# Layer 0: the two stores of each finished block of x1 go out on SyncE's queue instead of ScalarE's

## The chip, the cores and the metric

The kernel runs on one core of one Trainium2 chip. The metric is device time in microseconds (us): the median of three runs, 2891.63 us for the kernel before (2888.98 to 2893.01).

A core has five engines that run their own instruction streams and meet at semaphores: TensorE (PE; its weight loads are shown apart as PEld), VectorE (DVE), ScalarE (ACT), GpSimd (POOL) and SyncE (SP). In this kernel DMA transfers are issued from three of these streams: SP, ACT and POOL. An instruction that issues a DMA stands in its engine's stream like any other: what is written behind it on that engine waits for it to be issued.

## What is computed

The input x is (4, 16, 256, 256) float32: 4 images of 16 channels. Two layers follow each other, each with a residual:

```python
x = x + _L0_conv_ref(_gn(x), L0_conv_conv_w, L0_conv_conv_b)
x = x + _L1_conv_ref(_gn(x), L1_conv_base_weight, L1_conv_spline_weight,
                     L1_conv_spline_scaler, L1_conv_bias_weight)
```

`_gn` is a group normalization over 8 groups of 2 channels. Layer 0 computes, for each channel and pixel, 25 logits by a 3x3 convolution, a softmax over these 25, and the weighted sum of the 5x5 neighbourhood:

```python
out = conv_general_dilated(x, conv_w, padding='SAME') + conv_b
weights = softmax(out.reshape(N, C, 25, H, W), axis=2)
return einsum('ncuij,ncuij->ncij', unfold_5x5(x), weights)
```

Layer 1 is a 3x3 convolution over SiLU of its input and over eight cubic B-spline bases of it. It needs the group statistics of layer 0's result, called x1 here.

## The kernel before

**Layer 0** (`layer0`) works in strips: 128 image rows by 32 columns, all 16 channels; 4 images x 2 row halves x 8 strips = 64 strips. The variable n is the strip, j the column in it. A strip is done in 8 steps of 4 columns. In each step

- PE makes the logits of 4 columns with 2 matmuls for each (L974 from the tile am, L978 from an), 400 numbers per pixel, into PSUM tiles lg of two columns; three such tiles exist;
- ACT takes the exponential of each lg into a tile e (L997); four e tiles exist;
- POOL multiplies e with the pixels u (L1002) into e's second half;
- DVE sums both halves over the 25 neighbours into nd, numerator and denominator (L813), one step behind.

At the end of a strip nd becomes y, the quotient, on ACT (`seed`, L827 and L829: exp(-ln)) and DVE (`divide`, `refine`, `quotient`; L833, L837, L844). These small pieces are not done at once but put on a list with a number of steps to wait (`after`, `step`), so that they fall into later steps.

**Loads.** `load_im` brings am (four DMAs, L750) and an (one, L758) for 16 columns, half a strip; each has two buffers, so that a half's load waits until PE has finished the half before the one in hand. `load_u` (L771) brings u for a strip, `load_xc` (L791) the block's own x. All these are on SP's queue. Beside the strips the generator `normalize` prepares the next image: it loads xp (L321), normalizes on ACT (L373, L386), transposes on PE, and stores normalized rows and columns to DRAM on SP's queue (L329, L343; zero borders L312). One piece of it is drawn in each step with `next(ahead)`, after `step()`.

**The block of x1.** Four strips make a block of 128 columns (BS = 4), 16 blocks in all. When the last strip of a block has its quotient, `apply` adds y to xc with an accumulating DMA on POOL's queue (L851). Six steps later the statistics for layer 1 begin (`statistics`, L876: for each of 8 groups, one group a step, two activations with a running sum on ACT), and seven steps later `store` writes the block to DRAM, twice, since layer 1 reads x1 with its channels doubled: two DMAs of 1024 KB each (L913), in pieces of 512 bytes. For 15 of the 16 blocks they are on ACT's queue; for the last block (`n == len(strips) - 1`), which is finished strip by strip on POOL (L861), they are on POOL's. Counting the steps from the block's last strip n, the store falls into the step j = 12 of strip n + 3, on ACT behind the second group's statistics and ahead of that step's `seed` (L827).

**Order.** At the end of `layer0` a pass (`in_order`) ties every instruction to the one before it on the same engine, so each engine runs its instructions in the order in which they are written. On SP that is, around a store's step: the load_im called at j = 0; what `normalize` emits in the steps j = 0, 4, 8; the store's place, j = 12; what `normalize` emits there; then at j = 16 the next load_im, load_u and load_xc. Semaphores and the waits on them are made by the framework. Layer 1's instructions may begin behind marks near the end of layer 0 (`marks`; SP's is set at strip 60, ACT's at 61).

**Layer 1** (`layer1`) runs over 64 units of 16 rows: it loads x1 (xta, xtb, xtc, L1084; sla, slb, slc, L1097; yo, L1106) on SP's queue, computes spline features on ACT, DVE and POOL into ring, and the convolution on PE (L1304, L1313).

Of the kernel before, what the change touches and what calls it, by code (L numbers as in the profile page):

```python
# [34 lines left out]
def conv_preact_kernel(  # L35
# [12 lines left out]
    nc = tc.nc  # L48
# [430 lines left out]
    with tc.tile_pool(name="prep0", bufs=2) as prep, tc.tile_pool(  # L479
# [147 lines left out]
        for b in range(B):  # L627
            st = stat.tile([P, G, NH * (GC if b == 0 else 1), 6], F32, name=f"st0_{b}", tag=f"st0{min(b, 1)}")
            for hf in range(NH):
                n = b * NH + hf  # L630
# [90 lines left out]
    def layer0(shift):  # L721
# [4 lines left out]
        with tc.tile_pool(name=f"prep{arm}", bufs=2) as prep, tc.tile_pool(  # L726
# [11 lines left out]
            strips = [(b, hf, s) for b in range(B) for hf in range(NH) for s in range(NST)]  # L738
# [109 lines left out]
            def apply(n, y):  # L848
                xc = kept_blocks[n // BS]
                if not alone(n):  # L850
                    nc.gpsimd.dma_start(  # L851
                        xc.rearrange("p c w -> p (c w)"), y.rearrange("p c w -> p (c w)"),
                        accum_op=ALU.add,
                    )
                    for g in range(G):
                        after(6 + g, statistics, n, xc, g)
                    after(7, store, n, xc)
                    return
                w0 = n % BS * SW
                v = xc[:, :, w0 : w0 + SW]  # L860
                nc.gpsimd.tensor_add(v, v, y[:, :, w0 : w0 + SW])  # L861
                seeds[1:] = [newest(POOLE)]
                if n == len(strips) - 1:
                    store(n, xc)
                    after(1, last_statistics, n, xc)
# [40 lines left out]
            def store(n, xc):  # L906
                b, hf, s = strips[n]
                c0 = s * SW + SW - CX
                v = x1s[b][:, W : W + H * W].rearrange("c (p w) -> p c w", w=W)

                queue = nc.gpsimd if n == len(strips) - 1 else nc.scalar
                for h in range(2):
                    queue.dma_start(  # L913
                        v[hf * P : (hf + 1) * P, h * C : (h + 1) * C, c0 : c0 + CX], xc
                    )
# [521 lines left out]
```

## Time and profile before

The profile is one execution, 2885.0 us, its span (first to last instruction) 2883.2 us.

| what | before |
|---|---|
| median of 3 runs | 2891.63 us (2888.98 to 2893.01) |
| profiled execution / its span | 2885.0 / 2883.2 us |
| busy: PE, DVE, ACT, POOL | 2712.4, 2777.8, 2143.5, 2663.9 us |
| DVE, share of the span | 96% |
| SP's queue (q1): packets, MB, share of 16 DMA engines | 267876, 626.67, 70.2% |
| ACT's queue (q10): the same | 61920, 31.46, 3.8% |
| POOL's queue (q0): the same | 7664, 32.23, 5.4% |
| issues of x1s<-xc on ACT / on POOL | 30 / 2, 1024 KB each |

The page cuts the span into 40 slices of 72 us and gives the busy share of each engine in tenths:

```profile
PE   4699899999999999999999999996899999999998
DVE  7699899999999999999999999999999999999996
ACT  6566777667677567776665555647999999999995
POOL 4399899999999999999999999999899999999995
DMA  9877899879899778898886666766787878787883
```

Slices 1 and 2 are preparation (statistics of x, weights). Layer 0 follows, from about 123 us (POOL's first L1002) to about 2010 us (DVE's last L813), slices 2 to 28; the rest is layer 1. In layer 0 three engines, PE, DVE and POOL, are at 9 nearly everywhere, and ACT is at 5 to 7. A "9" is 90% or more: the row doesn't say which of the three has no time left. In the profile's lists of groups and waits, "L913 ACTq" is a DMA issue in ACT's stream; an idle time put down to "issue" is one in which the engine waited for nothing that the profile shows.

### The profile page before, as it was taken

The page shows a single profiled execution, that of the slowest core. Times are in us where ns is not written, and L with a number is a line of the kernel's source. Part 1 is how long each engine was busy: PE and PEld are TensorE (multiplying, and loading weights), DVE is VectorE, ACT ScalarE, POOL GpSimd, SP SyncE. Part 2 cuts the span into 40 slices and gives each one's busy share as a digit, 9 for nine tenths or more (in the row PEclk, how much of TensorE's full clock was granted, in tenths as well). Part 3 has the DMA queues.
Part 4 walks back from the last instruction along what each step waited for, and adds up shares of the span by engine and source line. Part 5 has one row for each costly group of instructions (what it writes and reads, how often), then busy time and mean ns, then how long its engine had stood idle before and what let it go on. Part 6 is the DMA issues. An engine that isn't in the chain of part 4 may idle for free.

```text
span 2883.2 us, 39200 instructions
## 1 busy us (share of the span) xinstructions
PE 2712.4 (94%) x14282; PEld 1499.2 (52%) x14282; DVE 2777.8 (96%) x1821; ACT 2143.5 (74%) x2737; POOL 2663.9 (92%) x1096
## 2 busy tenths in 40 slices
PE   4699899999999999999999999996899999999998
PEld 3466566666666666666666556664233343323222
DVE  7699899999999999999999999999999999999996
ACT  6566777667677567776665555647999999999995
POOL 4399899999999999999999999999899999999995
PEclk7799999999999999999999999998899999999999
DMA  9877899879899778898886666766787878787883
GB/s 286 258 230 228 265 283 294 265 225 270 248 283 272 237 218 245 252 290 246 250 252 186 198 191 192 205 207 203 221 261 239 260 244 258 237 264 244 256 246 104
DMA packets 337663, 692.96 MB, mean 240 GB/s; under 512 B 29554, under 2 KB 254276, under 8 KB 287092
## 3 DMA queue, kind: packets, MB, share of 16 engines
q1 hardware_dynamic: 267876, 626.67, 70.2%
q0 software_dynamic: 7664, 32.23, 5.4%
q10 hardware_dynamic: 61920, 31.46, 3.8%
q8 instruction: 115, 1.88, 0.3%
q14 instruction: 88, 0.72, 0.1%
HBM read 533.16 MB, written 121.15 MB: 227 GB/s over the span
## 4 chain that ended last, share of the span: by engine, by line
DVE 35%; PE 28%; POOL 11%; issue 10%; ACT 7%; DMA 6%; SPq 2%; DVEq 0%; ACTq 0%; POOLq 0%
DVE nd L813 25%; PE lg L974 13%; POOL e L1002 10%; PE yp L1304 9%; PE lg L978 4%; DVE ring L181 3%; DVE s L178 3%; PE yp L1313 2%; ACT xtb L1139 1%; DMA xtb<-x1s 1%; DVE r1a L1148 1%; ACT xta L1139 1%; DMA xin<-in_x_dram 1%; DMA xta<-x1s 1%; ACT xtc L1139 1%
## 5 line engine op out<-in xcount | busy, mean ns | idle before, releaser
L1002 POOL TENSOR_TENSOR e<-e,u 128x1600 f32<-128x1600 f32 x512 | 1804.8, 3756 | 70.7 <-ACT e L997 53.3
L974 PE MATMUL lg<-wm,am 128*128 128x400 f32 x4096 | 1737.3, 505 | 75.0 <-ACT e L997 61.8
L813 DVE TENSOR_REDUCE nd<-e 128x128 f32<-128x3200 f32 x512 | 1759.2, 3480 | 37.4 <-POOL e L1002 37.1
L978 PE MATMUL lg<-wn,an 96*128 96x400 f32 x2048 | 1350.7, 660 | 1.8 <-DMA an<-hsl 1.8
L997 ACT ACTIVATE e<-lg 128x800 f32<-128x800 f32 x1024 | 845.5, 839 | 576.0 <-PE lg L978 465.1
L974 PEld LDWEIGHTS lg<-wm,am 128*128 128x128 f32 x4096 | 766.8, 193 | 384.2 <-ACT e L997 79.8
L1304 PE MATMUL yp<-ring,wt 128*32 128x512 f32 x6144 | 721.2, 594 | 31.1 <-DVE ring L181 30.6
L978 PEld LDWEIGHTS lg<-wn,an 96*128 96x128 f32 x2048 | 389.3, 190 | 314.1 <-issue 10.5
L1304 PEld LDWEIGHTS yp<-ring,wt 128*32 128x32 f32 x6144 | 224.2, 109 | 494.6 <-issue 432.9
L1161 POOL TENSOR_TENSOR s1b<-s1b,r1a 128x1024 f32<-128x1024 f32 (+1 forms) x96 | 192.4, 2034 | 0.0
L1161 POOL TENSOR_TENSOR s1a<-s1a,r1a 128x1024 f32<-128x1024 f32 (+1 forms) x96 | 191.9, 2027 | 0.0
L181 DVE SCALAR_TENSOR_TENSOR ring<-s,s1a 128x1024 f32<-128x1024 f32 x132 | 156.7, 1212 | 0.9
L181 DVE SCALAR_TENSOR_TENSOR ring<-s,s1b 128x1024 f32<-128x1024 f32 (+1 forms) x128 | 153.8, 1227 | 0.3
L876 ACT ACTIVATE z<-xc,nrm 128x256 f32<-128x256 f32 x240 | 143.8, 599 | 4.0
L1161 POOL TENSOR_TENSOR s1a<-s1a,r1b 128x512 f32<-128x512 f32 (+2 forms) x68 | 119.3, 1778 | 0.0
L1161 POOL TENSOR_TENSOR s1b<-s1b,r1b 128x512 f32<-128x512 f32 x64 | 114.6, 1814 | 0.0
L178 DVE SCALAR_TENSOR_TENSOR s<-xta,cb,s 128x1024 f32<-128x1024 f32 (+2 forms) x90 | 112.4, 1274 | 0.5 <-DMA xtc<-x1s 0.4
L1157 POOL TENSOR_TENSOR s1a<-r1b 128x1536 f32<-128x1536 f32 (+1 forms) x31 | 86.5, 2790 | 24.9 <-ACT r1b L1146 24.9
L178 DVE SCALAR_TENSOR_TENSOR s<-xtb,cb,s 128x1024 f32<-128x1024 f32 (+2 forms) x85 | 107.3, 1289 | 0.4 <-ACT s L175 0.4
L178 DVE SCALAR_TENSOR_TENSOR s<-xtc,cb,s 128x1024 f32<-128x1024 f32 (+2 forms) x85 | 107.1, 1287 | 0.0
L175 ACT ACTIVATE s<-xta,cb 128x1024 f32<-128x1024 f32 (+2 forms) x90 | 96.4, 1085 | 12.4 <-DVE ring L181 11.0
L1157 POOL TENSOR_TENSOR s1b<-r1b 128x1536 f32<-128x1536 f32 (+1 forms) x32 | 86.2, 2695 | 20.5 <-ACT r1b L1146 20.5
(211 smaller groups left out, 2255.0 us busy)
## 6 DMA issues: line engine op xcount, KB each, us to landing
am<-hst SPq DMA_DIRECT2D x508, 259.8 KB
u<-hs SPq DMA_DIRECT2D x64, 1440.0 KB
an<-hsl SPq DMA_DIRECT2D x127, 519.5 KB
xta<-x1s SPq DMA_DIRECT2D x40, 1024.0 KB
xtb<-x1s SPq DMA_DIRECT2D x40, 1024.0 KB
xtc<-x1s SPq DMA_DIRECT2D x40, 1024.0 KB
x1s<-xc ACTq DMA_DIRECT2D x30, 1024.0 KB
hs<-hsp SPq DMA_DIRECT2D x32, 576.0 KB
```

Of the source, the lines that this page charges most:

```text
L175: nc.scalar.activation(s, t, AF.Square, scale=-0.5, bias=cb)
L178: nc.vector.scalar_tensor_tensor(p, t, cb2, s, ALU.subtract, ALU.mult)
L181: nc.vector.scalar_tensor_tensor(f, p, 0.0, q, ALU.min, op)
L813: nc.vector.tensor_reduce(nd[:, :, :, j : j + JG].rearrange("p t c j -> p t j c"), e.rearrange("p t j m c d -> p t j c m d"), AX.XY, ALU.add,)
L876: nc.scalar.activation(z, v, f, scale=nrm[b][:, 0, g : g + 1], bias=nrm[b][:, 1, g : g + 1], accum_out=st1[b][:, t, g, columns_of(n) : col ...
L974: nc.tensor.matmul(lg[:, i, :NL], lhsT=am[:, o : o + P], rhs=wm.rearrange("p m c d -> p (m c d)"), start=True, stop=False,)
L978: nc.tensor.matmul(lg[:, i, :NL], lhsT=an[:, o : o + P], rhs=wn.rearrange("p m c d -> p (m c d)"), start=False, stop=True,)
L997: nc.scalar.activation(ev, lg[:, :, :NL], AF.Exp)
L1002: nc.gpsimd.tensor_tensor(e[:, 1].rearrange("p j m c d -> p j (m c) d"), e[:, 0].rearrange("p j m c d -> p j (m c) d"), uv, ALU.mult,)
L1157: nc.gpsimd.tensor_tensor(s1(n, a, z), r1(n, a, z), r1(n, a, z), ALU.mult)
L1161: nc.gpsimd.tensor_tensor(s1(n, a, z), s1(n, a, z), r1(n, a, z), ALU.mult)
L1304: nc.tensor.matmul(yp[t * M : (t + 1) * M], lhsT=wt[:, d, e].rearrange("p r o -> p (r o)"), rhs=ring[:, r0 + t * RT + d : r0 + t * RT + d ...
```

## The change

```diff
@@ -908,7 +908,7 @@
                 c0 = s * SW + SW - CX
                 v = x1s[b][:, W : W + H * W].rearrange("c (p w) -> p c w", w=W)
 
-                queue = nc.gpsimd if n == len(strips) - 1 else nc.scalar
+                queue = nc.gpsimd if n == len(strips) - 1 else nc.sync
                 for h in range(2):
                     queue.dma_start(
                         v[hf * P : (hf + 1) * P, h * C : (h + 1) * C, c0 : c0 + CX], xc
```

The 30 stores of the first 15 blocks are issued in SP's stream. They move the same bytes between the same places, called in the same step of the program. The last block's two stay on POOL.

## The prediction

> **What bounds the kernel now.** I first read the cost groups, to see which engine of layer 0 has no time to spare. The columns are busy us, mean ns of one, then the idle time in front and who ended it.
>
> ```profile
> L1002 POOL TENSOR_TENSOR e<-e,u 128x1600 f32<-128x1600 f32 x512 | 1804.8, 3756 | 70.7 <-ACT e L997 53.3
> L813 DVE TENSOR_REDUCE nd<-e 128x128 f32<-128x3200 f32 x512 | 1759.2, 3480 | 37.4 <-POOL e L1002 37.1
> ```
>
> Both run once per four columns (a step) in about 3.5 us, so either could be the bound. The windows view of most of layer 0 decides: columns are busy time of PE, PEld, DVE, ACT, POOL, then clock and DMA share.
>
> ```profile
> 470.00:2000.00 1530.00, 1478.80 (x5183) 963.50 (x5181) 1520.18 (x601) 992.19 (x1625) 1495.38 (x464) 0.99 0.80 235
> ```
>
> DVE is idle for 1530.0 - 1520.2 = 9.8 us out of 1530, POOL for 35. The DVE timeline agrees: in a strip (8 steps) DVE has eight sums plus the three quotient operations (L833, L837, L844), together 28.94 us, which is what most strips last. **A stall of ACT, PE or POOL is therefore worth only what it makes DVE idle.** POOL's gaps are mostly its own spare time (8 x 3.48 = 27.9 against 28.94).
>
> Second, the store. The view by tile of xc (min/median/max ns), and ACT's timeline at the fifth block:
>
> ```profile
> L913 ACTq DMA_DIRECT2D x1s<-xc x30: 366/1074/5172, 313.2 to 1954.4; - x30
> ...
> 784.24 4.14 ACTq L913 DMA_DIRECT2D x1s<-xc  x2
> 784.74 0.19 ACT L876 ACTIVATION_READ_ACCUMULATOR z<-xc,nrm 128x1 f32 x1
> 788.43 0.60 ACT L827 ACTIVATE r<-nd 128x512 f32<-128x512 f32 x1 [3.50 <-issue]
> ...
> ACT r L827 <- issue: 49.9, 15, 5.0
> ```
>
> The first store of a pair issues in 0.37 us; the second holds ACT's queue for 1.76 to 5.17 us, and L827, which is next, starts when it lets go. Fifteen pairs cost ACT 49.9 us.
>
> Third, SP. Its waits (total, times, longest), and its timeline around the same store:
>
> ```profile
> SPq L750 <- PE lg L978: 845.2, 110, 12.8
> SPq L771 <- DMA x1s<-xc: 63.1, 11, 8.9
> SPq L343 <- DMA x1s<-xc: 44.3, 5, 13.9
> SPq L750 <- DMA x1s<-xc: 41.1, 10, 8.0
> ...
> 771.52 0.63 SPq L758 DMA_DIRECT2D an<-hsl  x1
> 776.80 0.38 SPq L321 DMA_DIRECT2D xp<-in_x_dram  x1
> 777.77 0.33 SPq L312 DMA_DIRECT2D hst<-zero  x1
> 782.11 9.00 SPq L750 DMA_DIRECT2D am<-hst  x4
> 791.22 1.20 SPq L758 DMA_DIRECT2D an<-hsl  x1
> 793.96 0.34 SPq L771 DMA_DIRECT2D u<-hs  x1
> ```
>
> SP mostly waits for PE to free an am buffer (845 us). It also waits 148 us for these stores, though am, u and hst read nothing of x1s: the records show eight completion semaphores taken in turn by the DMAs of both queues (the store at 784.24 and the am load issued at 790.60 carry the same one), so a late store holds a later load. Here the fourth am load comes 7 us after the third.
>
> **What the change removes.** All 15 pairs leave ACT: 49.9 us of stall. What that is worth is the idle time of DVE after each store. I asked DVE's waits in the 45 us after each of the 15 issues: in order 7.9, 3.0, 0, 0, 0.4, 0, 0, 0.7, 1.6, 2.0, 0, 0.5, 0, 0, 0. A typical one:
>
> ```profile
> 1243.02 17.05 DVE L813 TENSOR_REDUCE nd<-e 128x128 f32<-128x3200 f32 x5
> 1261.29 3.49 DVE L813 TENSOR_REDUCE nd<-e 128x128 f32<-128x3200 f32 x1 [1.21 <-POOL e L1002]
> ```
>
> Nine us after the store of 1250.5, DVE runs dry for 1.21 us; ACT had stood for 3.74, and queued e tiles covered the other 2.5. At seven other blocks cover was complete. In the first block not all is the store's. DVE's big gap there is 6.28 us; ACT waited 8.7 us for an xp load (L373) just before, which had used up the cover, and the store's share is its 3.74 us. The second (3.0) is loads held by the store's semaphore as much as ACT. The later ones sum to 0.44 + 0.71 + 1.63 + 2.25 + 0.54 = 5.6, with one small gap of the 1367.7 block just past the window, from DVE's timeline. Sum: 3.7 + 3.0 + 5.6 = **12.3 us**.
>
> A rule speaks against more than nothing: the Trainium skill, "DMA: Bandwidth & Descriptors", section "Issuing engines are not separate DMA queues", says that all issuers share the same 16 DMA engines, and that the choice of issuer saves only sequencer time, "usually small relative to the DMA itself". By the rule the edit is worth about 0. By the row the issue is not small: up to 5.2 us, while the packets of a pair end 8.4 to 11.9 us after its issue. I take the row for ACT's time and the rule for bandwidth: no byte moves faster.
>
> **What it adds on SP.** Thirty issues. By the step counters a block's store falls at column 12 of the strip after next but one, in program order behind the loads called at column 0 and ahead of those called at column 16 (am, an, u, xc). Three prices:
>
> (a) The wait for the accumulate of y into xc, which ACT paid earlier through its statistics. POOL issues it 23 to 33 us before today's store; it lands in
>
> ```profile
> DMA to landing us min/median/max: 8.8/12.7/14.3
> ```
>
> so at the latest some 9 us before, typically 11. SP has issued `an` 13 to 21 us before the store in 12 blocks (8 to 11 in three) and then has at most a few small DMAs (six column stores in four blocks) until PE frees the am buffer 2 to 3.5 us before it. So the wait lies inside SP's wait for PE: 0. If that cover failed, the next half's am, an, u and xc would all wait behind it, and PE for them.
>
> (b) Issue time: 0.37 + 1.76 us (ACT's rows where SP issued nothing at the same time), at most 0.37 + 5.17. With it the pair is done before PE's release in the eleven blocks without column stores, else about 2 us after it. A half takes PE 14 us, loads issue in 3.1 us, and an `an` load lands 5.7 us after issue (chain at 1026.61). So about 5 us are free: 0. Bounds: 0 to 15 x 2 us if nothing covered it.
>
> (c) Order of data. The same page, "Queues, rings and completion order", says that a DMA engine takes turns between queues but consumes each ring in order: am will now stand behind up to 2 MB of stores instead of alternating with them. By that rule, a pair issued 4 us before today's time in the worst blocks holds am's data to about +4.5, and it lands near +10 to +12 of today's store, where PE wants it at +12. By the row, today the semaphore makes it worse: at 1015.9 the am loads are issued at +5.8 to +10.1 and `an` lands at +16.4, PE waits, and DVE still has no idle time. So by both: 0 or a small gain. Elsewhere the stores run 5 to 11 us earlier than now and are over when am comes.
>
> Below nothing: the 148 us of SP's waits on stores mostly go. They cost DVE little today, already counted in block two.
>
> **The end of layer 0.** The last SP store moves to about 1942, the first load of layer 1 is at 1974. DVE waits 4.56 us at 2009.7 for ACT's last logarithm; ACT, free of a 3.95 us stall at 1954, may come earlier: gain 0 to 4.6. ACT is again paced by PE by then, so I take 0.
>
> What is late next is DVE itself, then the xp loads (idle at 300 to 312 and at 1700).
>
> **Sum.** -12.3 + 0 + 0, and I leave 1 us for small new gaps: -11.3. The profiled execution took 2885.0 us (span 2883.2), so its like is 2873.7 (span 2872). The median shown is 2891.6, within 0.3% of it; taken from that: **2880.3 us**. Its own range is 2873 to 2886.
>
> **Rivals.** *Hidden anyway.* DVE's gaps come back: statistics (16 activations of 0.6 us and their reads per block) overload ACT in the same steps, and PE's share of the cover is not larger. For it: blocks with a short second issue (1.76) still gave POOL gaps of 0.5 to 2.7. Against it: DVE had none there. With half or less of 12.3 returned: 2886 to 2892, say 2888.
>
> *Loads late behind the stores.* One queue, in order: the stores keep am, an and u back. Place: the first blocks (300 to 470), where DMA share is 0.94, and the four with six column stores ahead. It decides once the loads land more than 16.4 us after today's store time, which the trace shows to be harmless; that needs the pair's transfer to take 16 us or more rather than 8.4 to 11.9. Three blocks late by 2.7 us beyond that point make 8 us of DVE idle, and one more wait for xp like the first block's 6 us; less the 5.6 still gained at the later blocks, that is +8.4: 2900. Against it: SP's 845 us of waiting and the earlier issue.
>
> *The whole stall counts.* If POOL's and ACT's time were the bound, all 49.9 us would go: 2842. DVE's zero idle at seven stores speaks against it.
>
> *The change does nothing* is not open: only the last block's pair is on POOL, which stays.
>
> **Chances.** Forecast 0.60, hidden anyway 0.22, loads late 0.15, whole stall 0.03. A difference of under 0.2% (5.8 us) can't be told from no change here. Faster 0.63, same 0.22, slower 0.15. The range reaches from 2870 (12.3 + 4.6, and the 4 us by which runs differ) to 2896, most of the late-load case left out.
>
> **What would show it.** Right: no "issue" idle in front of L827; L913 on SP, issued 3 to 13 us before the matching ACT statistics; SP's waits for x1s<-xc near 0; DVE's gaps after stores gone, those at 300 to 312 and 1700 left; DVE's sums end near 1998 instead of 2009.7. Wrong: waits of PE for am or an, or of POOL for u, longer than now (8.0, 6.4 and 15.9 us); SP's store rows above 5 us; DVE idle in layer 0 not under 15 us (21.6 now); or layer 1 longer than 874 us from DVE's last sum to the end.

## The result, and the profile after

The changed kernel takes **2865.24 us** (median of four runs, 2861.58 to 2870.83), the kernel before, measured with it, 2890.31 us (2887.43 to 2893.01). The ratio is 0.9915, with a 95% interval of 0.9896 to 0.9934: 25.1 us faster, 19 to 30 by the interval. The forecast was 2880.3 us, 11.3 us faster. The profiled execution took 2861.6 us (span 2859.8, before 2883.2: 23.4 less); a second profiled execution of the same kernel, taken with the experiments, has a span of 2863.2 us (20.0 less). So two profiles of one kernel differ by 3.4 us here, and the four runs range over 9.

The issue itself went as foreseen. ACT's timeline at the fifth block no longer has the store; L827 follows the statistics at once. The columns are start, duration, then engine, line and tiles.

```profile
773.83 0.19 ACT L876 ACTIVATION_READ_ACCUMULATOR z<-xc,nrm 128x1 f32 x1
773.93 0.58 ACT L827 ACTIVATE r<-nd 128x512 f32<-128x512 f32 x1
```

The store stands in SP's timeline instead, 10 us before the place that it had beside these statistics:

```profile
759.29 0.68 SPq L758 DMA_DIRECT2D an<-hsl  x1
760.07 0.53 SPq L321 DMA_DIRECT2D xp<-in_x_dram  x1
760.65 0.50 SPq L312 DMA_DIRECT2D hst<-zero  x1
763.92 6.40 SPq L913 DMA_DIRECT2D x1s<-xc  x2
770.41 5.13 SPq L750 DMA_DIRECT2D am<-hst  x4
775.64 0.55 SPq L758 DMA_DIRECT2D an<-hsl  x1
776.29 0.53 SPq L771 DMA_DIRECT2D u<-hs  x1
```

The second issue of a pair is longer on SP than it was on ACT, 4.1 to 8.65 us (the view by tile: min, median, max ns over both issues of a pair), and all four am loads now follow without a break. SP has the time: its wait for PE in front of am stays in the hundreds of microseconds, and its 148 us of waits for the stores are gone from the list.

```profile
L913 SPq DMA_DIRECT2D x1s<-xc x30: 359/2754/8647, 295.5 to 1919.3; - x30
```

```profile
SPq L750 <- PE lg L978: 883.3, 110, 12.0
```

The costliest groups after. DVE's sums take as long as before; the idle time in front of them was 37.4 us and is 20.5, of which some 15 are the start of layer 0. ACT's idle time is now put down mostly to DVE.

```profile
L1002 POOL TENSOR_TENSOR e<-e,u 128x1600 f32<-128x1600 f32 x512 | 1806.0, 3818 | 45.0 <-ACT e L997 27.8
L813 DVE TENSOR_REDUCE nd<-e 128x128 f32<-128x3200 f32 x512 | 1757.9, 3489 | 20.5 <-POOL e L1002 20.5
L997 ACT ACTIVATE e<-lg 128x800 f32<-128x800 f32 x1024 | 810.3, 835 | 627.2 <-DVE nd L813 504.3
```

That last number is the main sign of what happened. ACT's waits in layer 0 (total us, times, longest), before:

```profile
ACT e L997 <- PE lg L978: 451.7, 548, 3.6
ACT e L997 <- DVE nd L813: 102.4, 69, 4.6
```

and after:

```profile
ACT e L997 <- DVE nd L813: 504.3, 333, 2.4
ACT e L997 <- PE lg L978: 100.1, 126, 2.2
```

Before, ACT mostly waited for PE to make a new lg: nothing lay ready in front of it. After, it mostly waits for DVE to free an e tile: all four e tiles are full. The work in hand ahead of DVE is a stock; it stood near empty and now stands near full.

**Where the microseconds went.** A strip without any loss takes DVE 28.94 us, from its first sum to the next strip's first sum. What a strip takes beyond this I call its excess; unlike the idle time that the profile names, it contains every loss. It is worked out from the starts of the 512 rows of L813.

| place | before | after | after, second execution | predicted gain | gain (mean of both) |
|---|---|---|---|---|---|
| strips 5 to 11 (first two stores) | 14.1 | 4.9 | 8.6 | 6.7 | 7.35 |
| strips 12 to 52 | 9.0 | 0.9 | 1.0 | 5.6 | 8.05 |
| strip 53 | 3.2 | 0.5 | 0.5 | 0 | 2.7 |
| last sum's start to the end of the run | 876.9 | 874.5 | 874.4 | 0 | 2.45 |
| ahead of the first sum | 126.5 | 125.6 | 125.5 | 0 | 0.95 |

The gains add up to 21.5 us, against 21.7 between the spans (mean of 23.4 and 20.0). The profiled execution of the kernel before is itself 5 us under that kernel's median, so 3.4 of the 25.1 us have no place in this table. The last row is not the change's: no store of x1 has been issued by then, and over the profiled executions of all runs this time lies anywhere between 121.5 and 128.7 us. Three of these places deserve a look at their rows.

*Strips 12 to 52.* The windows view of this stretch (length, then busy time of PE, PEld, DVE, ACT, POOL, then clock, DMA share, GB/s), before and after:

```profile
490.00:1650.00 1160.00, 1125.40 (x3967) 734.55 (x3967) 1153.81 (x440) 778.01 (x1293) 1135.01 (x348) 0.99 0.84 247
```

```profile
490.00:1650.00 1160.00, 1142.14 (x4006) 729.45 (x4005) 1159.54 (x446) 767.28 (x1295) 1147.26 (x351) 1.00 0.84 249
```

DVE's idle time falls from 6.2 to 0.5 us: 5.7, and the prediction said 5.6. But the excess falls by 8.05. The other 2.3 us were never shown as idle. In the kernel before, DVE's timeline has at 1273:

```profile
1273.27 6.87 DVE L813 TENSOR_REDUCE nd<-e 128x128 f32<-128x3200 f32 x2
1280.56 10.43 DVE L813 TENSOR_REDUCE nd<-e 128x128 f32<-128x3200 f32 x3 [0.42 <-POOL e L1002]
```

One sum lasts 3.49 us in its row; two that follow each other from a full stock take 6.87, so they start 3.38 apart. The three behind the gap take 10.43, so they start 3.47 apart, and no idle time stands between them: DVE follows POOL, which has just the next e ready. That is 0.09 us a sum that the idle column can't show.

*Strip 53.* The prediction put the idle time "at 1700" down to xp. The kernel before has there:

```profile
1683.30 17.05 DVE L813 TENSOR_REDUCE nd<-e 128x128 f32<-128x3200 f32 x5
1700.71 3.49 DVE L813 TENSOR_REDUCE nd<-e 128x128 f32<-128x3200 f32 x1 [0.36 <-POOL e L1002]
1704.11 0.68 DVE L833 TENSOR_TENSOR nd<-nd,r 128x512 f32<-128x512 f32 x1
1706.92 3.49 DVE L813 TENSOR_REDUCE nd<-e 128x128 f32<-128x3200 f32 x1 [2.13 <-POOL e L1002]
```

and the kernel after, in the same strip:

```profile
1665.14 20.47 DVE L813 TENSOR_REDUCE nd<-e 128x128 f32<-128x3200 f32 x6
1685.50 0.70 DVE L833 TENSOR_TENSOR nd<-nd,r 128x512 f32<-128x512 f32 x1
1686.10 3.51 DVE L813 TENSOR_REDUCE nd<-e 128x128 f32<-128x3200 f32 x1
```

POOL does a piece of image statistics there in both kernels (L206 and L207, 0.48 + 1.66 us before, 0.43 + 1.66 after). With a full stock DVE doesn't feel it; with an empty one it waits 2.5 us. The store that emptied it had been issued at 1601, 100 us earlier, far outside the 45 us that the prediction looked at.

ACT's stall of 5 us is not all that emptied it. All lg tiles were full, so PE stopped too, and behind that stop its granted clock was halved. PE's rows of L974 alone in the kernel before, around the store of 1601, and the windows view behind the stop (the clock is the number after the five busy times):

```profile
1602.92 0.84 PE L974 MATMUL lg<-wm,am 128*128 128x400 f32 x2
1608.85 1.70 PE L974 MATMUL lg<-wm,am 128*128 128x400 f32 x2 [4.91 <-ACT e L997]
1610.68 1.53 PE L974 MATMUL lg<-wm,am 128*128 128x400 f32 x2
1612.26 0.83 PE L974 MATMUL lg<-wm,am 128*128 128x400 f32 x2
```

```profile
1609.00:1612.50 3.50, 3.50 (x7) 2.13 (x8) 3.50 (x2) 2.55 (x7) 2.90 (x1) 0.55 1.16 356
```

The matmuls from 1608.85 to 1612.26 took 3.41 us, where the same work takes 1.71 right behind: PE loses 1.7 us of its lead just when it has to make it up. Between 480 and 1970 us the kernel before has nine such stretches of 3.4 or 6.8 us at half clock, the changed kernel none in either execution.

*The end of layer 0.* DVE's wait for ACT's last logarithm, before and after:

```profile
2014.26 0.69 DVE L833 TENSOR_TENSOR nd<-nd,r 128x512 f32<-128x512 f32 x1 [4.56 <-ACT r L829]
```

```profile
1990.04 0.69 DVE L833 TENSOR_TENSOR nd<-nd,r 128x512 f32<-128x512 f32 x1 [1.28 <-ACT r L829]
```

### The profile page after: what moved, and what is told of

It reads as the page before. It is cut to its first block, busy times and chain, and to the rows that moved or that the text cites. A ratio compares the mean times of both kernels' runs of the same rounds, so it can differ in the third digit from the quotient of the medians.

```text
span 2859.8 us, 39212 instructions
## 1 busy us (share of the span) xinstructions
PE 2716.4 (95%) x14282; PEld 1483.3 (52%) x14282; DVE 2774.1 (97%) x1821; ACT 2124.1 (74%) x2737; POOL 2666.5 (93%) x1096
## 4 chain that ended last, share of the span: by engine, by line
DVE 52%; PE 22%; issue 10%; ACT 6%; DMA 5%; POOL 2%; SPq 1%; DVEq 0%; POOLq 0%; ACTq 0%
DVE nd L813 42%; PE yp L1304 12%; PE lg L974 6%; PE yp L1313 3%; DVE ring L181 3%; DVE s L178 2%; PE lg L978 2%; DVE r L837 1%; DVE y L844 1%; DVE nd L833 1%; POOL e L1002 1%; DVE r1a L1148 1%; ACT xta L1139 1%; DMA xp<-in_x_dram 1%; ACT xtc L1139 1%
## 5 line engine op out<-in xcount | busy, mean ns | idle before, releaser
L1002 POOL TENSOR_TENSOR e<-e,u 128x1600 f32<-128x1600 f32 x512 | 1806.0, 3818 | 45.0 <-ACT e L997 27.8
L813 DVE TENSOR_REDUCE nd<-e 128x128 f32<-128x3200 f32 x512 | 1757.9, 3489 | 20.5 <-POOL e L1002 20.5
L974 PE MATMUL lg<-wm,am 128*128 128x400 f32 x4096 | 1731.6, 503 | 45.3 <-ACT e L997 33.3
L997 ACT ACTIVATE e<-lg 128x800 f32<-128x800 f32 x1024 | 810.3, 835 | 627.2 <-DVE nd L813 504.3
L974 PEld LDWEIGHTS lg<-wm,am 128*128 128x128 f32 x4096 | 750.7, 191 | 386.3 <-ACT e L997 113.1
```

The costliest lines, as they stand in the source:

```text
L813: nc.vector.tensor_reduce(nd[:, :, :, j : j + JG].rearrange("p t c j -> p t j c"), e.rearrange("p t j m c d -> p t j c m d"), AX.XY, ALU.add,)
L974: nc.tensor.matmul(lg[:, i, :NL], lhsT=am[:, o : o + P], rhs=wm.rearrange("p m c d -> p (m c d)"), start=True, stop=False,)
L997: nc.scalar.activation(ev, lg[:, :, :NL], AF.Exp)
L1002: nc.gpsimd.tensor_tensor(e[:, 1].rearrange("p j m c d -> p j (m c) d"), e[:, 0].rearrange("p j m c d -> p j (m c) d"), uv, ALU.mult,)
```

## The experiments

Two theories for a gain twice the forecast. **Theory A:** ACT's stall costs more than the idle time near it, because it drains the stock of ready e and lg tiles. The stock refills slowly (PE's matmuls start 3.43 us behind those of the step before in most steps and near 3.9 in about every ninth, DVE needs 28.94 / 8 = 3.62, so 0.1 to 0.2 us are gained a step), and later shortages are then paid. **Theory B:** SP's loads, held 148 us by the late stores, were the cost; the prediction put this near nothing. The gain could be A, B or both. All diffs are against the changed kernel unless another is named; "excess" is the sum over strips 0 to 62, "idle" is DVE's in the window 490 to 1650. Excess and idle are of the one profiled execution, the median of all runs of a kernel. The kernel before, measured again with each of the three groups of runs, had medians of 2890.89, 2888.62 and 2890.43 us, so a difference of 2 us between groups says nothing.

| run | median us | against after | excess | idle |
|---|---|---|---|---|
| before | 2890.31 | +25.1 | 30.8 | 6.2 |
| after | 2865.24 | | 10.9 | 0.5 |
| after again | 2865.16 | -0.1 | 14.5 | 0.4 |
| ACT held 2.7 us a block | 2872.18 | +6.9 | 24.5 | 0.4 |
| ACT held 4.5 us a block | 2890.96 | +25.7 | 40.6 | 12.3 |
| ACT held by the stall's own sizes | 2885.18 | +19.9 | 31.4 | 5.8 |
| ACT held once (one run) | 2865.04 | -0.2 | 13.5 | 0.4 |
| stores on ACT, in two steps | 2872.81 | +7.6 | 22.3 | 3.6 |
| one store on ACT, one on SP | 2874.72 | +9.5 | 23.0 | 4.2 |
| stores on ACT two steps later | 2893.39 | +28.2 | 39.1 | 14.5 |
| stores on SP, seven steps earlier | 2921.25 | +56.0 | 69.6 | 39.3 |
| stores on SP two steps later | 2871.48 | +6.2 | 17.6 | 1.2 |
| stores on SP, two steps apart | 2866.53 | +1.3 | 14.4 | 0.4 |
| stores on POOL | 2877.51 | +12.3 | 24.1 | 7.8 |

### ACT's stall put back without its store

The stores stay on SP. At their old place ACT does activations of 0.44 us each on 256 elements, which nothing reads, so that ACT is away for a known time while SP stays free. The first, with 2.7 us a block, 40 us in all:

```diff
+                if not alone(n):
+                    for h in range(6):
+                        z = x1p.tile([P, GC * CX], F32, name=f"hold_{n}_{h}{arm}", tag="z", bufs=1)
+                        nc.scalar.activation(z, wm.rearrange("p m c d -> p (m c d)")[:, 0:256], AF.Identity)
```

> The changed kernel (stores on SP), but ACT is kept busy where the stores stood before: six extra activations of 256 elements (about 0.5 us each, 3.1 us in all, results unused) behind each of the 15 stores. SP is free of any hold. Theory A (ACT's stall drains the stock of ready e and lg tiles, and the stock refills by only some 0.2 us a step, so that later shortages far from the store are paid by DVE too): DVE's idle time comes back at the old places: 4 to 8 us in strips 5 to 7, 1 to 2 us each near the stores of strips 34, 38, 42, 2 to 3 us in strip 53, and 3 us at the end of layer 0; DVE's idle in layer 0 15 us or more, span 2876 to 2886 (before 2883.2, after 2859.8). Theory B (the 148 us for which the stores' semaphores held SP's loads made the loss, by PE's lead): DVE idle stays near 5 us, span 2860 to 2866. In between, shares of both.

Measured: 2872.18 us (2869.32 to 2878.06), ratio to before 0.9937 (0.992 to 0.9953). Only 6.9 us come back for 40 us of hold, between the two theories. (The profiled execution is the slowest of the four, 2878.06 us, so its places add up to more.) In strips 12 to 52 the excess is 0.9 us, as in the changed kernel: 2.7 us fit wholly into the stock there. The cost is at the first two stores (17.6) and at the end (DVE waits 3.8 us for ACT's logarithm).

The same once only, at the store that falls into strip 50:

```diff
+                if n == 47:
+                    for h in range(6):
+                        z = x1p.tile([P, GC * CX], F32, name=f"hold_{n}_{h}{arm}", tag="z", bufs=1)
+                        nc.scalar.activation(z, wm.rearrange("p m c d -> p (m c d)")[:, 0:256], AF.Identity)
```

> As the run with ACT held at all stores, but held only once, about 3.1 us at the store in strip 50. Theory A: DVE is idle for 0 to 0.6 us there and for 2 to 3 us in strip 53, some 100 us later, where the drained stock has not refilled; the other places stay as in the changed kernel; span 2862 to 2865. Theory B or chance: strip 53 stays without idle time, span 2859 to 2861.

The time of one run, 2865.04 us, can't tell 1 us. The trace can. Strip 50 itself loses nothing, but three strips later, 100 us on, the gap is back:

```profile
1667.16 20.43 DVE L813 TENSOR_REDUCE nd<-e 128x128 f32<-128x3200 f32 x6
1687.52 0.67 DVE L833 TENSOR_TENSOR nd<-nd,r 128x512 f32<-128x512 f32 x1
1689.18 3.49 DVE L813 TENSOR_REDUCE nd<-e 128x128 f32<-128x3200 f32 x1 [0.99 <-POOL e L1006]
```

The excess of strip 53 is 1.6 us instead of 0.5, and no other strip from 12 on differs from the changed kernel's by over 0.1. So a stall of ACT is paid 100 us later, by an unrelated piece of work on POOL. PE stops for 2.66 us in this hold, and the one stretch of half clock between 480 and 1970 us, 3.4 us long, begins at its end; what the hold took and what the clock took of the stock can't be told apart in this run. (L1006 is L1002 with the added lines.)

Then ten activations a block, 4.5 us, 67 us in all:

```diff
-                    for h in range(6):
+                    for h in range(10):
```

> As the run with ACT held at all stores (six activations, which measured 2.7 us a block, 40 us in all, and cost 7.0 us of median against the changed kernel), with ten: some 4.5 us a block, 67 us in all, more than the 50 us of the kernel before (which had 1.5 to 5.0). Theory A (ACT's stall alone makes the loss, 25 us): the cost rises steeply with the size, interpolated to 50 us it should give 25, so here 35 or more: 2895 or above. Theory B (neither hold alone: ACT's stall counts because SP's loads are held by the stores' semaphores at the same time, so PE's lead can't refill): 10 to 16 us, 2875 to 2882, with no DVE idle time in strips 18 to 50, where the kernel before had 7.9 us.

Measured: 2890.96 us, ratio 1.0007 (0.9998 to 1.0015): as slow as the kernel before, though SP is free, and short of the 2895 that theory A had set. Strips 12 to 52 now cost 15.7 us where 2.7 us a block cost 0.9. The price of a stall is not linear: 2.7 us are free there, and of the 1.8 us more in each of ten holds, 18 in all, 14.8 are paid.

Because of this a fair test needs the stall's own sizes. In the kernel before they run from 1.76 to 5.17 us; the hold copies them in the order of the blocks, 50.6 us in all against 49.9:

```diff
-                    for h in range(10):
+                    for h in range([9, 4, 4, 7, 8, 9, 4, 9, 9, 11, 4, 11, 11, 7, 9][n // BS]):
```

> The changed kernel with ACT held at each store for as long as the kernel before was held there, block by block (4 to 11 activations, 1.7 to 4.8 us, 50.6 us in all; the kernel before: 1.5 to 5.0, 50 in all), and SP free. ACT's stall as such, without SP's held loads. Known: 40 us of even hold cost 7.0 us, 67 us cost 25.8; SP's hold without ACT's stall cost 7.6 to 9.5; both together (kernel before) 25. If the two costs add: 25 - 8 = 15 to 18 us here, median 2880 to 2883. If they only count together: under 10 us, 2872 to 2875. If the stall were all of it: 2888 or above.

Measured: 2885.18 us (20 runs, 2879.28 to 2890.19), ratio 0.9982 (0.9975 to 0.9988). **ACT's stall alone is worth 19.9 of the 25 us** (20.0 against the changed kernel measured with it), more than the 15 to 18 expected. It includes what PE's half clock adds: this run has nine such stretches between 480 and 1970 us, as the kernel before. Place by place it rebuilds the kernel before: strips 12 to 52 cost 8.2 us (before 9.0), strip 53 3.3 (3.2). Its windows row and its wait at the end:

```profile
490.00:1650.00 1160.00, 1128.49 (x3972) 734.60 (x3970) 1154.21 (x440) 806.54 (x1370) 1135.94 (x348) 0.99 0.84 248
```

```profile
DVE nd L833 <- ACT r L829: 4.5, 1, 4.5
```

ACT's waits are turned back too, without one store in its stream:

```profile
ACT e L1001 <- PE lg L982: 389.2, 483, 2.2
ACT e L1001 <- DVE nd L813: 154.2, 102, 4.7
```

### SP's held loads without ACT's stall

From the kernel before: both stores stay on ACT, but one step apart.

```diff
-                    after(7, store, n, xc)
+                    for h in range(2):
+                        after(7 + h, store, n, xc, (h,))
...
-            def store(n, xc):
+            def store(n, xc, halves=(0, 1)):
...
-                for h in range(2):
+                for h in halves:
```

> The kernel before, both stores on ACT, but the second one a step (3.6 us) behind the first instead of straight behind it. The first issue of a pair took 0.37 us and held nobody; if the second then also finds its queue free, ACT's stall is under 0.3 us a block, while SP's loads are held by the stores' semaphores as before (100 to 150 us of SP waits on x1s<-xc). Theory A (ACT's stall is the loss): 2863 to 2869, as the changed kernel (2865.2). Theory B (half of it and more is SP's hold, and PE waits for am and an): 2872 to 2880, with PE's waits for am and an 15 to 30 us in layer 0. If the second issue holds ACT even so, its length says what it waits for.

Measured: 2872.81 us, ratio 0.9945 (0.9928 to 0.9963). ACT's stall is gone (an issue takes 0.37 us, at most 1.4), and SP's waits for the stores are there as before:

```profile
L914 ACTq DMA_DIRECT2D x1s<-xc x30: 366/367/1417, 310.6 to 1948.0; - x30
```

```profile
SPq L750 <- DMA x1s<-xc: 59.4, 7, 11.6
SPq L771 <- DMA x1s<-xc: 58.4, 7, 9.2
SPq L343 <- DMA x1s<-xc: 7.8, 1, 7.8
```

The 7.6 us over the changed kernel (8.7 by the two ratios to the kernel before) are what the held loads cost here. PE waits for them, where the changed kernel has 3.0 and 0.8 behind the start of layer 0:

```profile
PE lg L975 <- DMA am<-hst: 15.9, 7, 4.2
PE lg L979 <- DMA an<-hsl: 8.8, 14, 1.7
```

They reach DVE at strips 23 and 39 (1.65 and 1.72 us) and at the first stores (13.0 us against 4.9 and 8.6). With the sized hold this adds to 27.5, against 25.1 together: the two causes nearly add, A 2.6 times B. But in the profile of the kernel before PE waits only 0.3 us for am and 1.8 for an behind the start of layer 0: where ACT's stall holds PE as well, the held loads hardly reach it. (With the stores on ACT two steps later, further down, SP stands 73 us for them, and PE waits for no am load.)

The other mixture has the first store of a pair on ACT and the second on SP:

```diff
-                    queue.dma_start(
+                    (nc.scalar if h == 0 and queue is nc.sync else queue).dma_start(
```

> One store of each pair on ACT, the other on SP. If only a second issue behind a first on the same queue holds an engine, ACT's stall is under 0.3 us a block, and under theory A the span is that of the changed kernel, 2857 to 2863. If the two queues' issues share one generator, ACT's store holds ACT for about 1.5 us when SP's is issued just ahead of it: stall up to 23 us, span 2862 to 2870. Theory B: a store late on ACT holds SP's loads again, span 2866 to 2876.

Measured: 2874.72 us, ratio 0.995 (0.9933 to 0.9966). One late store a pair is enough to hold SP (56.5 us at L771, 25.2 at L750), and PE waits 19.1 us for am. It agrees with the run before.

### How much room the stores have

On ACT two steps later, behind the column-16 loads (from the kernel before):

```diff
-                    after(7, store, n, xc)
+                    after(9, store, n, xc)
```

> The kernel before (stores on ACT), with the stores two steps later (9 steps behind the accumulate instead of 7), about 7 us later, where SP should not be issuing loads. If the second issue takes 1.76 us when SP issues nothing beside it and 3.5 to 5.2 when it does, ACT's stall falls from 49.9 to about 23 us in all. Theory A: DVE idle falls to 6 to 12 us and the span to 2862 to 2872. Theory B (SP's loads are still held by the stores' semaphores, now those of the next half): span 2876 to 2886.

A miss: the issues did not get short. Measured 2893.39 us, ratio 1.0009 (1.0002 to 1.0016). They meet SP's u and xc loads there and last 4.3 to 7.6 us. The stall only moves in front of other instructions of ACT:

```profile
ACT e L997 <- issue: 37.0, 7, 7.4
ACT hsp L373 <- issue: 9.4, 2, 5.0
ACT ht L386 <- issue: 9.2, 2, 4.7
```

On SP right behind the accumulate, where the cover of the prediction's price (a) is gone:

```diff
-                    after(7, store, n, xc)
+                    after(0, store, n, xc)
```

> The changed kernel with the stores written one step behind the accumulate instead of seven, so that SP reaches them before the accumulate has landed: SP waits for it (landing 12 us after its issue) with the next half's am and an loads queued behind. This takes away the cover on which the prediction's price for the wait on SP rests. Expected: SP's waits on xc<-y 8 to 12 us a block, the loads of a half 4 to 8 us later than PE frees their buffer; with ACT never held PE's lead covers most of it: 2865 to 2872 (theory A) or 2870 to 2880 (theory B: SP's hold costs by itself).

A miss by 40 us: 2921.25 us, ratio 1.0105 (1.0088 to 1.0123). SP stands before the store until y has landed in xc, and the next half's loads stand behind it:

```profile
SPq L913 <- DMA xc<-y: 192.0, 14, 14.2
```

```profile
PE lg L974 <- DMA am<-hst: 64.3, 11, 9.5
```

So a wait on SP does cost, once it outlasts SP's wait for PE; at the place of the change that same wait is 5.0 us in all.

On SP two steps later:

```diff
-                    after(7, store, n, xc)
+                    after(9, store, n, xc)
```

> The changed kernel with the stores two steps later on SP, behind the next half's am, an, u and xc loads rather than ahead of them. If the order of loads and stores on SP's queue still costs anything (PE's waits for am and an are 3.8 us in the changed kernel), 1 to 4 us faster: 2861 to 2864. If SP's spare time already hides the pair: 2863 to 2867. It is slower only if the stores then meet the following half's loads: above 2867.

A miss too: 2871.48 us, ratio 0.994 (0.9923 to 0.9958), 6.2 us behind the changed kernel. Right behind SP's u and xc loads the first store of a pair takes long too, 6.7 to 8.1 us in twelve blocks, and PE waits 10.7 us for am and 3.4 for an. In the profiled execution, though, 3.2 of the 5.9 us behind the second one of the changed kernel lie ahead of the first sum, where no store is yet; 3.1 lie in the strips. So an end of the room on this side is likely, not shown.

On SP with the second store two steps behind the first (`after(7 + 2 * h, store, n, xc, (h,))`):

> The changed kernel with the two stores two steps apart on SP, one ahead of the next half's loads and one behind. The second issue should then no longer take 4 to 8.6 us: near 0.4 to 1.5. As the 5 us lie in SP's wait for PE, no effect on the time: 2863 to 2867; up to 3 us faster if part of them wasn't hidden.

Measured: 2866.53 us, ratio 0.9928 (0.9911 to 0.9945), no different from the changed kernel. The issues did not get short as expected: the second lasts 6.9 to 9.6 us in twelve blocks. Long issues on SP cost nothing there.

On POOL:

```diff
-                queue = nc.gpsimd if n == len(strips) - 1 else nc.sync
+                queue = nc.gpsimd
```

> All stores on POOL, as the last block's are: neither ACT nor SP is held by them, and their semaphores are of another set. POOL pays about 1.2 us for each issue (its rows in the profile before), 2.4 us a block, against spare time of about 1 us a strip. Both theories: ACT's stall 0 and SP's waits on x1s<-xc near 0, span within 4 us of the changed kernel (2859.8), median 2863 to 2870; above 2872 only if POOL's 36 us count.

A miss: 2877.51 us, ratio 0.9955 (0.9937 to 0.9973). An issue takes POOL 1.2 to 4.6 us (median 2.3), and POOL has less to spare than SP: from 250 us on DVE waits 16.7 us for it, 5.1 and 8.4 in the two executions of the changed kernel.

And the changed kernel once more, for the scatter of a profile:

> The changed kernel again, unaltered, on the chip of the other three: 2862 to 2868. Its trace shows how far the excess of the first strips (2.3 us in strip 6, 2.2 in strip 11) differs between executions: within 3 us of these.

Measured: 2865.16 us, ratio 0.9919 (0.9902 to 0.9936). Strips 5 to 11 cost 8.6 us instead of 4.9, the rest is the same to 0.1 us. Differences under 4 us in the first two blocks are therefore not read in any of these runs. No run was clearly faster than the changed kernel.

## Why the prediction was right in direction and wrong in size

- **Right:** the bound (DVE), the mechanism (stores leave ACT, its "issue" idle is gone), and that the new place on SP is covered. The waits put 49.9 us on L827 before and none after. PE's waits for loads, one mark of the forecast, say little: of its 8.0 us for am 7.7 were the start of layer 0, and its 6.4 for an were the weight loads'. Behind that start PE's matmuls waited 0.3 us for am and 1.8 for an before, 3.0 and 0.8 after; the weight loads' waits for an fell from 6.4 to 3.3.
- **Right:** "12.3 us" of visible idle time near the stores. Strips 12 to 52 gave 5.7 of the 5.6 expected. That the first two blocks gave 7.35 of 6.7 is luck in part: it is the mean of 9.2 and 5.5 in two executions.
- **The step that failed:** "What that is worth is the idle time of DVE after each store." ACT's stall alone is worth 19.9 us by the sized hold. The idle time in a 45 us window leaves out what the stall, and the half clock of PE behind it, do to the stock. (How the two share it no run tells: none holds ACT with PE's clock kept.) Missing were 2.3 us in strips 12 to 52 that no idle column shows, 2.7 us at strip 53, 100 us behind the store ("those at 300 to 312 and 1700 left": the one at 1700 went), and 2.4 us at the end of the layer. The last had a step of its own, "ACT is again paced by PE by then, so I take 0", inside bounds of 0 to 4.6; the sized hold shows the wait of 4.5 us to be ACT's stall.
- **The second term mis-sized:** SP's 148 us of waits, "They cost DVE little today, already counted in block two". By the stores in two steps they cost 7.6 us alone. How much of this they added on top of ACT's stall is less sure: the medians of the kernel before and of the sized hold differ by 5.2 us (3.5 to 7.2 by the interval), their two profiled spans by nothing, and PE's waits of 0.3 and 1.8 us in the kernel before don't show them. So "little" may have been right for the kernel as it stood; the rest of the 25 us beyond ACT's 19.9 stays without a place.
- The reserve of 1 us for new gaps was not needed. Idle time at 300 to 312 is gone in one execution and back in the other (2.5 us in strip 5), so it says nothing of the change. DVE's last sum ended at 1988.8 and 1992.3 us, ahead of the forecast's 1998.
- **The rule of the Trainium skill** ("DMA: Bandwidth & Descriptors", "Issuing engines are not separate DMA queues") that the choice of issuer saves only issue time, "usually small", would have made it about 0. The prediction was right to side with the row against it: the saved issue time is worth 20 us here. The page's other half holds: the DMA share of the window 490 to 1650 stays at 0.84.
- One sign was set wrongly. "SP's store rows above 5 us" was to prove the forecast wrong; they reach 8.65 us, beyond the 5.17 that the prediction's price (b) took for the most, without harm, since SP's wait for PE is longer.
- Of the rivals, "hidden anyway", "loads late" and "the whole stall counts" (2842) all fell. The first two only came about where a run made them: with 2.7 us a block in strips 12 to 52, and with the store on SP too early.

## What to carry to other kernels

When the bounding engine is fed through a few buffers, the idle time next to a stall is only the lower bound of its cost: look at which way the feeder's waits point (for its source: the stock is empty; for its consumer: it is full), and compare start-to-start times of the bounding instruction with its best stretch. If the stock is empty most of the time, count later gaps with unrelated releasers as part of the stall's price. A hold of known length at the stall's place, in the stall's own sizes, measures that price; a hold of the mean size does not, since up to the stock's depth it costs nothing. Look at the granted clock behind such a stall as well: here it fell to half for 3.4 to 6.8 us where the stall had stopped PE.

## What was not expected of the hardware

The second of two store issues in a row takes a time that depends on what has been issued before it, also from the other engine. On ACT it lasted 1.76 to 1.83 us at the four blocks where SP had issued nothing for 3.6 us or more, and 3.5 to 5.2 us at the others; on SP, behind its own loads, 4.1 to 8.65, but 1.65 to 2.9 in the run seven steps earlier, where SP had stood waiting for xc; on ACT behind SP's u and xc loads 4.3 to 7.6; with one step between the two, 0.37, at most 1.4. The traces don't show what the issue waits for. A late store on one queue also held loads of another that share nothing with it but, by the records, the completion semaphore: SP stood 152 us for it in the kernel before (148 in the prediction's three rows), 128 with the stores in two steps, and 119 with one store of each pair on ACT.
